# An expert layer on one core: all nodes at once in tiles of 256 rows, against two halves of the nodes in tiles of 128 rows

## The chip, the cores and the metric

The kernel runs on one core of one Trainium2 chip. The metric is the device time of one execution of the whole program, in microseconds (us). Three unprofiled runs of the kernel before took 3043.54, 3038.19 and 3040.16 us; their median, 3040.16, is the time before. The engines are named as in the profile: PE (TensorE matmul), PEld (TensorE weight load), DVE (VectorE), ACT (ScalarE), POOL (GpSimd) and SP (SyncE, which here only issues DMAs). A line number such as L1242 is a line of the kernel before, unless it is said to be of the changed kernel.

## What is computed

The input is a matrix x of 4096 nodes by 256 features and a 4096 x 4096 adjacency matrix. Layer 0 is a graph attention with 4 heads and a feed-forward part of 30 repeated steps; layer 1 is two graph attentions and then a mixture of experts. The change touches only this last part, and everything ahead of it stays as it was. Cut to that part, the reference is:

```python
n = layernorm(x)                                     # 4096 x 256
rh = relu(n @ router_w1 + router_b1)                 # 256 -> 128
p = softmax(rh @ router_w2 + router_b2)              # 128 -> 6 experts
top_w, top_i = top_k(p, 2)                           # two experts a node
w = softmax(top_w)
h1 = relu(n @ expert_w1[e] + expert_b1[e])           # each 256 x 256
h2 = relu(h1 @ expert_w2[e] + expert_b2[e])
y[e] = h2 @ expert_w3[e] + expert_b3[e]
x = x + w[0] * y[top_i[0]] + w[1] * y[top_i[1]]
```

The reference computes all six experts for every node; the kernel computes only the two that a node chose. All of it is in float32 except where the routing counts and compares small whole numbers.

## The kernel before, in words

P is 128, C is 256, KC is C/P = 2, E is 6 experts, G is 4. The 4096 nodes are 32 blocks of 128 (NT) or 8 groups of G x 128 = 512 nodes (NG, GR). The instructions are put in order on each engine by a scheduler that follows the order of the program's text as far as tiles and buffers allow; each engine then works through its own queue in order, and waits are semaphores. The expert stage (L938 to L1322) has three parts, one after the other.

**Routing.** The loop over groups (L971) is written as a pipeline. For a group it takes the rows of x (loaded by SP), finds mean and variance on DVE and the power -1/2 on POOL (`over_std`, L95 to L106), writes the normalised n on DVE (L992), stores n to the DRAM matrix nd through SP (L995), transposes n on PE into fT (L113, copied by ACT at L997), runs the router's two layers on PE (`ps_r` L981 with rh on ACT at L983, `ps_l` L1004), and adds the bias to the logits lg on DVE (L1007). ACT also keeps the group's rows in acc (L998), the sum that the outputs will be added to. After the eighth group SP issues the expert weights (18 transfers of 256 KB, L1016) and the last bias (L1017). Then some forty small DVE operations over all 32 blocks (L1054 to L1130) take the softmax, find the two best experts (`lmax`, `tot`, `top`, `hot`, `at`), count with matmuls by matrices of ones how many nodes each expert has ahead of a given one (`any` L1082, L1089 to L1092), find how many tiles each expert needs (`many` L1099), and give each of the 8192 pairs of node and choice a place in a list in which the pairs of one expert stand together and each expert begins at a new tile (`mine` L1121, then `pos`, `hi`, `lo`). The list is turned round by one-hot matrices: for four blocks of 16 x 128 pairs DVE writes `ohl` (L1137) and `ohh` (L1141, L1144), and PE multiplies them (L1147, 16 matmuls a block). From the product come `source`, the row of nd for each place (L1164), and `dest`, the row of yd (L1165). DVE then finds the expert of each tile (L1168 to L1176), the biases of its two hidden layers (`ohe`, `sel`, `bsel`, L1178 to L1188), and the two weights of each node (`ws`, L1191 to L1195).

**Tiles.** A tile is TR = 256 places of the list; T = 2 x 4096/256 + 5 = 37 tiles are enough for any choice of the nodes. For tile i:

- `gather`: POOL issues two indirect DMAs of 128 rows each from nd into gx (L1207; 4 buffers).
- `turn`: PE transposes gx into `pt` (L1219, 4 transposes), DVE copies it to xT (L1221).
- `fetch`: PE, DVE and ACT read the tile's expert number into a register (L1225); DVE copies that expert's first weight matrix and ACT the second to a fixed place (L1235).
- `hidden`, layers 0 and 1: PE multiplies (L1242, 4 matmuls of 256 columns a layer; the trace shows a float32 matmul as two records); relu with bias is on ACT for layer 0 (L1253) and on DVE for layer 1 (L1255).
- `result`: PE multiplies by the third matrix (`po`, L1263), DVE adds the bias (`ye`, L1271), and POOL issues two indirect DMAs that write the 256 rows to their places in the DRAM matrix yd (L1273).

The text interleaves two tiles, so that PE has another tile's work between two dependent steps:

```python
for i in range(T + 1):
    gather(i + 2)
    fetch(i + 1)
    hidden(i, 0, ...)      # PE, then ACT
    result(i - 1)          # PE, then DVE, then POOL
    turn(i + 1)            # PE, then DVE
    hidden(i, 1, ...)      # PE, then DVE
```

**Combine.** When all tiles are written, SP reads yd back in 16 transfers of 512 KB into y (L1308; 8 buffers), DVE adds each block of 128 rows, times its weight, to acc (L1319, 64 operations), and ACT issues the output of each group (L1322).

One row from outside the stage is spoken of too: L519 is the inner matmul of the attention (16-bit, 130 columns, a weight load for each), which is the last thing that runs ahead of this stage.

Of the kernel before, what the change touches and what calls it, by code (L numbers as in the profile page):

```python
# [11 lines left out]
F32 = mybir.dt.float32  # L12
# [11 lines left out]
P = 128  # L24
# [22 lines left out]
def gnn_ffn_kernel(ctx: ExitStack, tc: tile.TileContext, a: dict, out: bass.AP):  # L47
# [890 lines left out]
    with ExitStack() as scope:  # L938
        T = 2 * N // TR + E - 1
        T2 = 2 * T  # L940
# [4 lines left out]
        bsel = one.tile([P, T, 2 * KC], F32, name="bsel")  # L945
        expert = one.tile([P, T], I32, name="expert")
        dest = one.tile([P, T2], I32, name="dest")
        source = one.tile([P, T2], I32, name="source")
        ew = [one.tile([P, E, KC, C], F32, name=f"ew{i}") for i in range(3)]
        b3 = one.tile([P, E, C], F32, name="b3")  # L950
        nd = dram.tile([N, C], F32, name="nd")
        yd = dram.tile([2 * N + T * TR, C], F32, name="yd")

        with ExitStack() as rs:
            work = rs.enter_context(tc.tile_pool(name="r_work", bufs=2))
            rone = rs.enter_context(tc.tile_pool(name="r_one", bufs=1))
            psum = rs.enter_context(tc.tile_pool(name="r_ps", bufs=1, space=PSUM))
            ps_t = rs.enter_context(tc.tile_pool(name="r_pst", bufs=2, space=PSUM))

            def bank(name):  # L960
                return psum.tile([P, 512], F32, name=name)

            ps = bank("ps_s")
            nc.tensor.transpose(ps[:, :NB], br, ident[:NB, :NB])
            nc.vector.tensor_copy(bT, ps[:, :NB])

            lg = rone.tile([P, NT, E], F32, name="lg")
            rows, stds, fTs, rhs = {}, {}, {}, {}


            for g in range(NG + 2):  # L971
                if g + 2 < NG:
                    load_ahead(x3d, g + 2, runs_of)
                if g < NG:
                    rows[g] = ahead.pop(g)
                    stds[g] = over_std(work, rows[g])
                if 2 <= g:
                    ps = bank("ps_r")
                    fT = fTs.pop(g - 2)
                    for k in range(KC):  # L980
                        nc.tensor.matmul(ps[:RH], rw1[:, k, :], fT[:, k, :], start=(k == 0), stop=(k == KC - 1))  # L981
                    rh = rhs[g - 2] = work.tile([RH, GR], F32, name="rh")
                    nc.scalar.activation(rh, ps[:RH], AF.Relu, bias=bT[:RH, 0:1])  # L983
                if 1 <= g <= NG:
                    u = g - 1
                    t = rows.pop(u)
                    rstd, mv = stds.pop(u)
                    nmr = work.tile([P, G], F32, name="nmr")
                    nc.vector.scalar_tensor_tensor(nmr, mv[:, :, 0], -1.0, rstd, op0=OP.mult, op1=OP.mult)
                    n = work.tile([P, G, C], F32, name="n")  # L990
# [4 lines left out]
                    nc.sync.dma_start(runs_of(nd, u), n)  # L995
                    fT = fTs[u] = work.tile([P, KC, GR], F32, name="fT")
                    nc.scalar.copy(fT, transposed(ps_t, n))  # L997
                    nc.scalar.activation(acc[:, u * G : (u + 1) * G, :], t, AF.Identity, bias=mone)  # L998
# [14 lines left out]
            for i in range(3):  # L1013
                src = a[f"L1_ffn_expert_w{i + 1}"]
                for e in range(E):
                    nc.sync.dma_start(ew[i][:, e], src[e].rearrange("(k p) f -> p k f", p=P))  # L1016
            nc.sync.dma_start(b3, bcast_rows(a["L1_ffn_expert_b3"]))  # L1017

            def numbers(name, pattern, base, step, dtype=F32):
                shape = [P] + [n for _, n in pattern]  # L1020
                ti = rone.tile(shape, I32, name=f"{name}_i")
                nc.gpsimd.iota(ti, pattern=[list(x) for x in pattern], base=base, channel_multiplier=step)
                tf = rone.tile(shape, dtype, name=name)
                nc.gpsimd.tensor_copy(tf, ti)
                return tf

            HB = NT // 2
            along = numbers("along", [(1, max(T, N // TR))], 0, 0)
            along16 = numbers("along16", [(1, P), (0, HB)], 0, 0, F16)
            place = numbers("place", [(P, T2)], 2 * N + GR, 1)  # L1030


            code = rone.tile([P, 2, NT, 2], F16, name="code")
            nc.gpsimd.tensor_copy(code[:, :, :, 0], numbers("code0", [(0, 2 * NG), (1, G)], 0, G).rearrange(
                "p (i g) r -> p i (g r)", i=2))
            nc.gpsimd.tensor_copy(code[:, :, :, 1], numbers("code1", [(1, 2 * NG), (0, G)], 1, 0).rearrange(
                "p (i g) r -> p i (g r)", i=2))
            words = code.rearrange("p i t w -> p (i t w)").bitcast(F32).rearrange("p (i t) -> p i t", i=2)
            before = rone.tile([P, P], F32, name="before")
            nc.gpsimd.memset(before, 1.0)  # L1040
            nc.gpsimd.affine_select(
                before, before, pattern=[[1, P]], compare_op=OP.is_gt, fill=0.0, base=0, channel_multiplier=-1
            )
            before16 = rone.tile([P, P], BF16, name="before16")
# [242 lines left out]
        for i in range(T + 1):  # L1287
            if i + 2 < T:
                gather(i + 2)
# [63 lines left out]
```

## Time and profile before

| | |
|---|---|
| unprofiled runs | 3043.54, 3038.19, 3040.16 us; median 3040.16 |
| profiled execution, whole | 3026.16 us |
| its span, first to last instruction | 3024.4 us |
| mean granted clock of TensorE | 0.970 |
| busy PE, PEld | 2812.5 us (93%), 2549.3 us (84%) |
| busy DVE, ACT, POOL | 2709.9 us (90%), 2422.3 us (80%), 1167.0 us (39%) |
| expert stage in the trace | about 2690 to 3024.4 us |
| the list of rows to gather (`source`) complete | 2763.8 us |
| first gather; first hidden layer | 2764.80; 2772.2 us |
| first read of yd issued | about 2988.0 us |

The profile comes from one execution. Its times count from the first instruction; the whole is 1.8 us longer than the span. The busy shares are means over the whole program, most of which is the attention and the feed-forward part; the expert stage is its last tenth, so its limits have to be read from that stretch alone. The granted clock is the TensorE clock that the throttle gave, as a share of full speed. Matmuls are pipelined and the ends of the records are modelled, so the step from one record to the next is the length of a group of n records less the duration of one, divided by n - 1. A wait's releaser is inferred from semaphores, and where several semaphores are waited for, the one that came last by the profile is named.

### The profile page before, as it was taken

What the parts mean: (1) busy time and instruction counts of PE and PEld (TensorE: products, weight loads), DVE (VectorE), ACT (ScalarE), POOL (GpSimd) and SP (SyncE); (2) the same over time, 40 slices, a digit from 0 to 9 for tenths busy, and PEclk for the clock granted to TensorE, in tenths of its full rate; (3) what the DMA queues carried; (4) which work ended last, traced back from release to release, by engine and by line L of the source; (5) the groups of instructions that cost most, each with busy time, mean ns of one, the idle gap of its engine ahead of it and who ended that gap; (6) DMA issues with size and microseconds to landing.
All of it is one profiled execution on the core that took longest, in us unless ns stands there. A gap on an engine that the chain in (4) does not pass through costs nothing. (4 is left out here: it accounts for less than half of the span.)

```text
span 3024.4 us, 80903 instructions
## 1 busy us (share of the span) xinstructions
PE 2812.5 (93%) x33327; PEld 2549.3 (84%) x33327; DVE 2709.9 (90%) x5529; ACT 2422.3 (80%) x3011; POOL 1167.0 (39%) x1056
## 2 busy tenths in 40 slices
PE   6899999979999999999998999999799999985994
PEld 5899999958888888888877999999689999974883
DVE  8999999989999999999998899999689999985445
ACT  6799999788888888888867999999689999951220
POOL 2000000089999999999992000000200000022672
PEclk9999999989999999999999999999999999997997
DMA  9998884153333333333333022120302223142225
GB/s 291 273 247 242 231 247 114 33 134 68 68 68 69 67 67 70 68 67 69 69 100 109 29 93 85 41 89 16 106 27 86 71 92 93 30 137 76 95 93 200
DMA packets 482889, 319.96 MB, mean 106 GB/s; under 512 B 416573, under 2 KB 443354, under 8 KB 476378
## 3 DMA queue, kind: packets, MB, share of 16 engines
q1 hardware_dynamic: 467698, 287.13, 35.6%
q0 software_dynamic: 7680, 21.51, 2.2%
q10 hardware_dynamic: 7144, 6.16, 0.7%
q8 instruction: 263, 4.31, 0.6%
q14 instruction: 104, 0.85, 0.1%
HBM read 183.00 MB, written 52.04 MB: 78 GB/s over the span
## 5 line engine op out<-in xcount | busy, mean ns | idle before, releaser
L519 PE MATMUL acc<-vals,st 128*128 128x130 f16 x12288 | 1433.7, 219 | 35.7 <-DVE u L472 27.5
L519 PE MATMUL acc<-vals,below 128*128 128x130 f16 x12288 | 1433.3, 221 | 12.3 <-DVE below L573 11.7
L461 ACT ACTIVATE st<-f1b,nf 128x1024 int8<-128x1024 f32 x1265 | 1334.3, 1142 | 32.1 <-PE acc L519 22.7
L519 PEld LDWEIGHTS <-below 128*128 128x128 fp8e4 x12288 | 1177.1, 96 | 48.7 <-issue 44.1
L519 PEld LDWEIGHTS <-st 128*128 128x128 fp8e4 x12288 | 1208.8, 98 | 9.5 <-DVE st L567 7.5
L863 PE MATMUL po<-wT,zT 128*128 128x256 f32 x1920 | 576.0, 382 | 7.7 <-ACT zT L846 6.5
L866 PE MATMUL po<-w,zT 128*128 128x256 f16 x3840 | 577.7, 273 | 0.3 <-DMA zT<-z 0.3
L827 POOL TENSOR_TENSOR th<-th,y 128x1024 f32<-128x1024 f32 x240 | 567.6, 2365 | 26.8 <-ACT th L826 4.4
L866 PEld LDWEIGHTS <-zT 128*128 128x128 f16 x3840 | 376.3, 98 | 161.6 <-DMA zT<-z 1.3
L573 DVE TENSOR_TENSOR below<-m,st 128x1024 int32<-128x1024 int32 x384 | 469.9, 1224 | 32.7 <-DVE st L567 1.2
L567 DVE TENSOR_TENSOR st<-st,m 128x1024 int32<-128x1024 int32 x384 | 466.9, 1216 | 1.1 <-ACT st L461 0.9
L803 DVE SCALAR_TENSOR_TENSOR y<-po,z_rs,bias 128x256 f32<-128x256 f32 x928 | 384.4, 476 | 2.2 <-PE tp L796 0.7
L839 DVE BATCH_NORM_STATS2 z_st<-z 128x6 f32<-128x256 f32 x960 | 335.5, 411 | 0.0
L863 PEld LDWEIGHTS po<-wT,zT 128*128 128x128 f32 x1920 | 290.8, 192 | 17.7 <-ACT zT L846 9.3
L815 ACT ACTIVATE z<-th 128x1024 f32<-128x1024 f32 x240 | 251.0, 1046 | 8.6 <-POOL th L827 8.3
L826 ACT ACTIVATE th<-y 128x1024 f32<-128x1024 f32 x240 | 250.1, 1042 | 0.1
L105 POOL TENSOR_TENSOR ln_rstd<-ln_rstd,mhalf 128x4 f32<-128x4 f32 x24 | 32.0, 1334 | 562.0 <-ACT acc L998 491.8
L850 POOL TENSOR_TENSOR z_rs<-z_rs,mhalf 128x4 f32<-128x4 f32 x240 | 245.0, 1021 | 0.0
L846 ACT COPY zT<-tp 128x512 f32<-128x512 f32 x240 | 140.4, 585 | 110.3 <-PE tp L796 110.2
L459 DVE TENSOR_SCALAR st<-f1b,nf 128x1024 int8<-128x1024 f32 x271 | 200.9, 742 | 6.8 <-PE acc L519 6.8
L436 POOL MEMSET hs<- 128x4 f32 x3 | 0.3, 101 | 490.6 <-DVE u L489 490.6
L818 DVE SCALAR_TENSOR_TENSOR z<-z,scale,z 128x512 f16<-128x512 f32 x240 | 179.0, 746 | 4.9 <-ACT z L817 4.9
(237 smaller groups left out, 2815.4 us busy)
## 6 DMA issues: line engine op xcount, KB each, us to landing
adj<-in_adj_dram SPq DMA_DIRECT2D x64, 1024.0 KB
m<-edges SPq DMA_DIRECT2D x32, 1024.0 KB
f1b<-fd SPq DMA_DIRECT2D x48, 512.0 KB
edges<-m SPq DMA_DIRECT2D x16, 1024.0 KB
y<-yd SPq DMA_DIRECT2D x16, 512.0 KB
ew<-in_L_ffn_expert_w_dram SPq DMA_DIRECT2D x18, 256.0 KB
t<-in_x_dram SPq DMA_DIRECT2D x8, 512.0 KB
old<-in_x_dram SPq DMA_DIRECT2D x16, 256.0 KB
```

The source lines that it names most:

```text
L461: nc.scalar.activation(out, f1, AF.Sign, bias=f2, scale=-1.0)
L519: nc.tensor.matmul(acc[:, i, cols], masked[part][:, at_i // TR, s, rows], v[:, cols], start=(j == 0 and part == 0), stop=(j == NT - 1 and ...
L567: nc.vector.tensor_tensor(above, above, whole, OP.bitwise_and)
L573: nc.vector.tensor_tensor(below, whole, above, OP.bitwise_xor)
L803: nc.vector.scalar_tensor_tensor(y[:, g * G + r, :], po[:, r, :], rstd[:, r : r + 1], last if end else bias, op0=OP.mult, op1=OP.add,)
L815: nc.scalar.activation(z, th.pop(u), AF.Silu, scale=0.01)
L826: nc.scalar.activation(th[at], y[:, g * G : (g + 1) * G, :], AF.Tanh, scale=0.01)
L827: ins = nc.gpsimd.tensor_tensor(th[at], th[at], y[:, g * G : (g + 1) * G, :], OP.add)
L839: nc.vector.bn_stats(st[:, r, :], z[:, r, :])
L850: nc.gpsimd.tensor_tensor(rs[u], rs[u], mhalf, OP.pow)
L863: nc.tensor.matmul(po[:, r, :], src[:, r * P : (r + 1) * P], wT, start=True, stop=False)
L866: nc.tensor.matmul(po[:, r, :], src16[:, part * G + r, :], w16[:, other, :], start=False, stop=(part == 1 and other == 1),)
```

## The change

The nodes are cut into two halves of 2048 (NH), each of which has its own list, its own nd and yd, its own `source`, `dest`, `expert` and `bsel`. A tile becomes 128 places, so that a half has T = 2 x 2048/128 + 5 = 37 tiles, and both together 74. The stage's parts become:

- `route(h, ...)` is the routing of one half, written as a generator that stops at 20 places (`yield`). The half has 4 groups, 16 blocks, one-hot operations in two blocks instead of four, and about half as many elements in the small DVE operations. The constants that the routing needs are made once on POOL, ahead of it. The route of half 0 runs ahead of the tiles; after its first four steps SP issues the expert weights, so that they stand in SP's queue ahead of the stores of that half's last two groups.
- The route of half 1 takes one step after each tile of half 0 (`i < T - 2`); what is left of it is taken before the first gather of half 1.
- `combine(h)` is a generator too. That of half 0 takes one step after each tile from tile T + 5 on; what is left of it, and the combine of half 1, follow the tiles.
- In the tiles a gather, and a scatter, is one indirect DMA instead of two; `turn` has 2 transposes instead of 4, a layer of `hidden` has its 4 matmuls with 128 columns instead of 256, and `po` has 2 matmuls of 256 columns instead of 4. The w copies and the register reads stay as large as they were, so there are twice as many of them in all.
- Buffers: gx has 6 (of half the size) instead of 4, `ph` has 1 for each layer instead of 2, the second routing has a pool of one buffer for each of its two tiles in PSUM (`tp` and `ps`), and y has 4 instead of 8.

In the changed kernel's own queues, the gather of tile i + 8 stands next to the scatter of tile i on POOL; the four pow operations of the second routing stand between gathers 2 and 3, 3 and 4, 7 and 8, and after the first scatter. On DVE a tile is ye of tile i - 1, xT of i + 1, the register read and w copy of i + 2, then the two halves of h1 of i; the six one-hot operations of the second routing stand in one row ahead of a ye, and the first weighted sum of the first combine stands after xT of tile 40. ACT's four output issues of that combine stand after h0 of tiles 41, 43 and later ones.

The diff, cut to its core:

```diff
-        T = 2 * N // TR + E - 1
-        T2 = 2 * T
+        NH, NTH, NGH = N // 2, NT // 2, NG // 2
+        T = 2 * NH // P + E - 1
...
+        bsel = [one.tile([P, T, 2 * KC], F32, name=f"bsel{h}") for h in range(2)]
+        expert = [one.tile([P, T], I32, name=f"expert{h}") for h in range(2)]
+        dest = [one.tile([P, T], I32, name=f"dest{h}") for h in range(2)]
+        source = [one.tile([P, T], I32, name=f"source{h}") for h in range(2)]
...
+        nd = [dram.tile([NH, C], F32, name=f"nd{h}") for h in range(2)]
+        yd = [dram.tile([2 * NH + T * P, C], F32, name=f"yd{h}") for h in range(2)]
+        rwork = scope.enter_context(tc.tile_pool(name="r_work", bufs=2))
+        rone = scope.enter_context(tc.tile_pool(name="r_one", bufs=1))
...
+        def route(h, turned, bank):
+
+            lg = rone.tile([P, NTH, E], F32, name="lg")
...
+                    yield
+                if 1 <= g <= NGH:
...
+                    yield
...
+            for i in range(2):
+                ohh = rwork.tile([P, T, NTH], F32, name="ohh")
...
+                ohl = rwork.tile([P, P, NTH], F16, name="ohl")
...
+                        start=(i == 0 and t == 0),
+                        stop=(i == 1 and t == NTH - 1),
...
+            steps = route(0, turned, bank)
+            for _ in range(4):
+                next(steps)
+            for i in range(3):
+                src = a[f"L1_ffn_expert_w{i + 1}"]
+                for e in range(E):
+                    nc.sync.dma_start(ew[i][:, e], src[e].rearrange("(k p) f -> p k f", p=P))
+            nc.sync.dma_start(b3, bcast_rows(a["L1_ffn_expert_b3"]))
+            for _ in steps:
+                pass
...
-        ps_h = scope.enter_context(tc.tile_pool(name="m_psh", bufs=2, space=PSUM))
+        ps_h = scope.enter_context(tc.tile_pool(name="m_psh", bufs=1, space=PSUM))
         ps_o = scope.enter_context(tc.tile_pool(name="m_pso", bufs=2, space=PSUM))
+        ps_r = scope.enter_context(tc.tile_pool(name="m_psr", bufs=1, space=PSUM))
         rows, xT, hT, which, held = {}, {}, {}, {}, {}
-        scatters = []
+        scatters = [[], []]
...
         def gather(i):
-            rows[i] = work.tile([P, 2, C], F32, name="gx", bufs=4)
-            for r in range(2):
-                nc.gpsimd.indirect_dma_start(
-                    out=rows[i][:, r, :],
-                    out_offset=None,
-                    in_=nd[:, :],
-                    in_offset=bass.IndirectOffsetOnAxis(ap=source[:, 2 * i + r : 2 * i + r + 1], axis=0),
-                )
+            h, t = divmod(i, T)
+            rows[i] = work.tile([P, C], F32, name="gx", bufs=6)
+            nc.gpsimd.indirect_dma_start(
+                out=rows[i],
+                out_offset=None,
+                in_=nd[h][:, :],
+                in_offset=bass.IndirectOffsetOnAxis(ap=source[h][:, t : t + 1], axis=0),
+            )
...
+            for k in range(KC):
+                nc.tensor.matmul(po, src[:, k, :], w[:, 0, k, :], start=(k == 0), stop=(k == KC - 1))
...
+            y = work.tile([P, C], F32, name="ye")
+            nc.vector.tensor_tensor(y, po, b3[:, bass.DynSlice(which[i], 1)].rearrange("p o c -> p (o c)"), OP.add)
...
+        def combine(h):
+            ys = {}
+            for g in range(NGH + 2):
+                if g < NGH:
+                    ys[g] = []
+                    for i in range(2):
+                        ys[g].append(work.tile([P, G, C], F32, name="y", bufs=4))
+                        nc.sync.dma_start(ys[g][i], runs_of(yd[h], i * NGH + g))
+                    yield
+                if 2 <= g:
+                    at = (h * NGH + g - 2) * G
+                    for i, y in enumerate(ys.pop(g - 2)):
+                        for r in range(G):
+                            t = at + r
+                            nc.vector.scalar_tensor_tensor(
+                                acc[:, t, :], y[:, r, :], ws[:, i, t : t + 1], acc[:, t, :], op0=OP.mult, op1=OP.add
+                            )
+                        yield
+                    nc.scalar.dma_start(runs_of(out, h * NGH + g - 2), acc[:, at : at + G, :])
...
+        second = route(1, ps_r, lambda name: ps_r.tile([P, 512], F32, name="ps"))
         gather(0)
         gather(1)
-        for i in range(T + 1):
-            if i + 2 < T:
+        for i in range(2 * T + 1):
+            if i + 2 < 2 * T:
+                if i + 2 == T:
+                    for _ in second:
+                        pass
+                    second = combine(0)
                 gather(i + 2)
...
+            if i < T - 2 or i > T + 4:
+                next(second, None)
+        for _ in second:
+            pass
+        for _ in combine(1):
+            pass
```

## The prediction

> **What bounds the kernel now.** I read the page's slices first: only the last tenth of the span concerns this change, so I cut that tenth into stages with the table of busy time by stretch. Its columns are the stretch, its length, and busy time (instructions) of PE, PEld, DVE, ACT and POOL, then the granted clock, DMA share and GB/s.
>
> ```profile
> 2690.00:2729.00 39.00, 35.30 (x160) 21.91 (x160) 23.49 (x103) 18.17 (x21) 14.99 (x29) 0.88 0.82 283
> 2729.00:2744.50 15.50, 0.69 (x4) 0.27 (x4) 14.05 (x45) 0.59 (x2) 0.00 (x0) 0.53 0.07 27
> 2744.50:2764.80 20.30, 8.94 (x64) 8.31 (x64) 16.77 (x21) 0.77 (x2) 0.00 (x0) 0.58 0.00 0
> ...
> 2785.00:2983.00 198.00, 197.42 (x982) 173.40 (x980) 93.33 (x172) 49.52 (x103) 129.92 (x133) 1.00 0.28 89
> ...
> 2988.00:3024.40 36.40, 0.00 (x0) 0.00 (x0) 26.01 (x64) 0.00 (x0) 0.00 (x0) 0.50 0.88 346
> ```
>
> The reader is to see three serial stages: routing (to 2764.8), tiles (PE busy 197.4 of 198 us), and combine (DMA and DVE, no PE). Routing and combine leave PE nearly idle, but the tiles leave PE no room at all. The chain that ended last (start, length, what) gives the joints:
>
> ```profile
> 2727.64 1.07 PE ps_l L1004 x8
> ...
> 2744.54 1.30 DVE ohh L1141
> ...
> 2759.80 2.24 PE ps_r L1147 x16
> 2764.80 1.13 POOL gx L1207
> ...
> 2772.62 7.82 PE ph L1242 x24
> ...
> 2985.49 2.41 DMA yd<-ye,dest
> 2988.04 3.63 DMA y<-yd
> ...
> 3019.72 0.79 DVE acc L1319 x2
> ```
>
> In the tiles the chain runs over POOL's gathers and scatters, but each gather there waits for "PE pt"; the timeline of PE shows who leads. One tile of 256 rows:
>
> ```profile
> 2855.12 0.60 PE L1219 MATMUL pt<-ident,gx 128*128 128x128 f32 x4
> 2855.56 1.89 PE L1242 MATMUL ph<-h,w 128*128 128x256 f32 x8
> 2857.29 1.89 PE L1242 MATMUL ph<-xT,w 128*128 128x256 f32 x8
> 2859.02 1.89 PE L1263 MATMUL po<-ew,h 128*128 x8
> 2860.74 0.60 PE L1219 MATMUL pt<-ident,gx 128*128 128x128 f32 x4
> ```
>
> From pt to pt is 5.62 us, without a gap. One record's step is (group length − one duration)/(count − 1): (1.89 − 0.379)/7 = 0.216 for 256 columns, (0.60 − 0.273)/3 = 0.109 for a transpose of 128. DVE beside it:
>
> ```profile
> 2855.32 0.69 DVE L1271 TENSOR_TENSOR ye<-po,b 128x512 f32<-128x512 f32 x1 [1.16 <-DMA yd<-ye,dest]
> 2855.93 0.68 DVE L1221 COPY xT<-pt 128x512 f32<-128x512 f32 x1
> 2857.49 0.88 DVE L1255 TENSOR_SCALAR h<-ph,bsel 128x256 f32<-128x256 f32 x2 [0.88 <-PE ph L1242]
> 2859.22 0.56 DVE L1235 COPY w<-ew 128x512 f32 x1 [0.85 <-PE ph L1242]
> ```
>
> DVE works 2.8 of 5.62 us. ye starts 0.20 after po's last slot: with "DMA yd" named but PE just done, this wait is PE's.
>
> **The change, step by step** (on the profiled execution: span 3024.4, whole 3026.16 us).
>
> 1. Routing ahead of the tiles, now for half the nodes. The fourth group's lg stands at 2712.93, the eighth's at 2728.74: −15.8. Of the small DVE operations, some 16 of 192 elements (0.36) become 96 (0.26, as many L1099), and any and mine lose half of 1.0 and 0.87: −2.4; one w copy now stands among them, +0.6. The one-hot run, 2744.46 to 2759.74, was four blocks of 2 × 1.30 + 1.14; two blocks of 2 × 0.68 + 1.14 take 5.0: −10.3. Behind the one-hots the order by engine puts the second half's first statistics (4 × 0.35 + 3 × 0.1) between the list's last steps: +1.7. Sum **−26.2**. On SP, all 18 expert weight loads and the bias (5.5 MB) now precede two of the four nd stores. At 200 to 280 GB/s (the first stretch moved 283) they end near 2713, the stores a few us later, some 20 us before the first gather: nothing.
>
> 2. From the list to the first hidden layer: 8.4 us before (2763.8 to 2772.2). One gather less is needed for tile 0 (−1.4), but PE's queue has the transpose of tile 3 ahead of tile 0's second layer, and POOL now has a pow (1.05 + 0.30) between gathers 2 and 3. I take **0**, ends −2 and +4.
>
> 3. Tiles: 74 of 128 rows instead of 37 of 256, as many rows (9472), gathers (74) and scatters (74). Per tile PE has 16 hidden records of 128 columns, not in the trace as such. Below stands half of 0.216 = 0.108; above, each record's own weight load: L1004's, with 6 columns to stream, step (1.06 − 0.254)/7 = 0.115. I take 0.111: 1.78. po: 4 × 0.216 = 0.86; pt: 2 × 0.109 = 0.22. Sum 2.86, × 74 = 211.6 against 37 × 5.62 = 207.9: +3.7. The handovers do not halve. DVE after po's end: 0.20 to ye, 0.35 and 0.33 to get through ye and xT, some 0.2 for the register read (0.30 long) that the w copy needs, 0.49 for that copy, then h: first half ready at 1.92, and PE's weight load takes 0.18 more (first po: h at 2779.62, 0.48 long, po at 2780.28). PE's next po could start at 0.22 + 0.89 + 0.89 = 2.00. I charge 0.09 a tile: 2.95, +6.7. POOL needs 2 × (0.97 + 0.30) = 2.55 and stays under it. Sum **+10.4**; ends −1 (0.108, no wait) and +29 (3.20).
>
> 4. The second half's routing, placed among tiles 0 to 20. PE: per group 8 × 0.109 + 4 × 0.43 (L981) + 8 × 0.111 = 3.48, × 4 = 13.9; one-hots 32 × 0.14 = 4.5; counts 0.5. PE has no idle time there, so 18.9 is on the path: it is moved, not hidden. DVE: half of 23.5 + 14 + 16.8, with less saved on fixed costs, some 31 us. Idle DVE is about 1.0 a tile × 37 plus the time under PE's 18.9, so it fits by sum, but the queue is in order: the six one-hot operations (5.0) stand in a row ahead of a ye (+3), sel and bsel (0.99 each) ahead of h (+2), the counts wait for DVE (+1), small ones around xT (+3): +9. ACT's extra (four acc 1.15, eight fT 0.6, four rh 0.69) has room: it works under half of a tile. The four pow cost POOL 5.4 of its 14 idle us. Sum **+27.9**; ends +18.9 and +38.
>
> 5. The first half's combine, among tiles 39 to 47. 32 operations, 28 of which took 11.24 before: 0.40 each, 12.8 in 8 tiles, 1.6 a tile against 1.0 idle, partly ahead of h: +6. The first waits for its read: the last scatter (2.4 to land), then 3.6, while its place in DVE's queue is about two tiles after that po; what is queued behind it is h, and PE behind h: +3. SP has only later reads behind its wait; ACT's four output issues stand after h0 and before the next w copy. Sum **+9**; ends 0 and +15.
>
> 6. The end. The read back of one half: the first 8 of the 16 reads were used up by 3005.4 (the ninth group's wait ends at 3007.73), 17.4 after 2988.04, and then an output of 3.6 follows: 21.0 instead of 36.4, **−15.4**. Buffers fall from 8 to 4; with four in flight DVE (1.6 a read) still frees one before the next is due. Ends −18 and −11.
>
> Sum: −26.2 + 0 + 10.4 + 27.9 + 9 − 15.4 = **+5.7**: span 3030.1, whole 3031.9. The unprofiled runs had a median of 3040.16, 14.0 above the profiled one; I add the same difference: **3045.9**.
>
> Two rules of the Trainium skill speak against the change. In the L519 stream 479 records took 27.80 us, 0.058 each with a weight load for every 130 columns. "TensorE: Matmul & The Clock Gate", Back-to-back issue gap, gives 81 ns sustained at 128 columns against 56 isolated; by that surplus, 16 records × 25 ns would add an estimated 30 us to step 3. The row is this kernel's, so I leave it out. The w copy took 0.41 alone and 0.565 at the median among gathers, while those kept to 0.96 to 0.99: it is DVE that waits. "SBUF — State Buffer", the "DVE blocks DMA" trap, has it the other way: such a copy keeps GpSimd from writing descriptors; an estimated 0.43 on POOL's 2.55 would bound a tile at 2.98, 2 us more in all.
>
> **Rivals.** *Faster: the fillers fit.* DVE's 31 us and the combine go entirely into idle DVE time, and tiles run at 2.86. For it: idle time suffices by sum, and before, ye to h has 0.88 idle. Against it: the in-order blocks. −26.2 + 3.7 + 18.9 + 2 − 16 = −17.6: 3022.6. It decides if tiles 22 to 36 step at 2.9 or less and steps 4 and 5 lose under 5 us beyond PE's 18.9. *Slower: handovers bound the tile.* PE waits for h or xT in every tile because their latencies stay while the cover (0.89 instead of 1.73) halves; at 3.20 a tile step 3 grows by 18.5: +24, 3064. For it: my chain ends within 0.1 of PE's. It decides from about 3.05 on. *It doesn't do what it says:* the second list might end after tile 36 and hold gather 37. Its last steps are queued near tile 20, so 16 tiles (47 us) are spare; under 1 in 50, counted with slower.
>
> **How the numbers follow.** Chances: forecast 0.50, faster rival 0.28, slower rival 0.22. A measurement tells about 0.2%, 6.1 us, from no change. The forecast's own spread is ±8 around +5.7: of its 0.50, some 0.04 is faster, 0.23 within, 0.23 slower; its own range is 3038 to 3054. The faster rival gives 0.25 and 0.03, the slower 0.22. Faster 0.29, same 0.26, slower 0.45. The range takes in most of both rivals: 3024 to 3068.
>
> **What would show it.** Step 1: first gather near 2738. Step 3: pt to pt of 2.95 in tiles 50 to 70, hidden records at 0.111. Step 4: first to last po of the first half 28 us over 37 tiles' time, PE's gaps before h around the one-hots. Step 5: DVE idle before acc on "DMA y", stretched tiles 39 to 47. Step 6: 21 us from the last read's issue run to the end. I am wrong if hidden records step at 0.13 or more (weights not under the stream), or if PE falls to a lower granted clock between tiles, as it did after its idle time at 2764 (0.68 in that stretch).

## The result and the profile after

The changed kernel took 3031.83 us (median of 11 runs, 3027.09 to 3037.21) against 3040.16 (11 runs, one of which, 3312.09, stands far off): ratio 0.9972, 95% interval 0.9962 to 0.9982. It is faster by 8.3 us, where 5.7 slower was forecast; the time lies in the stated range, the sign is the other one. Its profiled execution has a span of 3033.0 and took 3034.78. So the two profiled executions stand the other way round than the medians: 3024.4 before, 3033.0 after. That contradiction is the first thing that had to be cleared up.

The table of busy time by stretch of the changed kernel; its columns are those of the prediction (stretch, length, busy time and instructions of PE, PEld, DVE, ACT, POOL, granted clock, DMA share, GB/s):

```profile
2713.00:2734.50 21.50, 3.08 (x36) 2.61 (x35) 19.59 (x72) 6.03 (x8) 0.00 (x0) 0.50 0.04 14
...
2741.60:2800.00 58.40, 58.23 (x392) 51.20 (x393) 35.49 (x118) 25.42 (x56) 31.53 (x32) 0.96 0.31 102
...
2919.00:2979.00 60.00, 55.63 (x394) 50.78 (x393) 31.63 (x90) 20.01 (x53) 35.34 (x36) 0.97 0.26 86
...
3010.00:3033.00 23.00, 0.00 (x0) 0.00 (x0) 13.11 (x32) 0.00 (x0) 0.00 (x0) 0.50 0.73 274
```

The reader is to see the same three kinds of stage, with the first and the last shortened (the list is ready at 2733.4, and only 32 sums follow the tiles), and a new thing in the third line: tiles with nothing placed among them, in which PE works 55.6 of 60 us. Before, that stretch had 197.4 of 198. The chain that ended last has the joints:

```profile
2734.55 1.13 POOL gx L1224
...
2883.87 3.84 DMA yd<-ye,dest
2887.73 3.28 DMA y<-yd
...
3007.53 2.41 DMA yd<-ye,dest
3010.88 6.20 DMA y<-yd
```

The first half's last scatter and first read now lie on the chain in the middle of the tiles (2883.87, 2887.73), the second half's at the end.

In PE's timeline, the starts of successive `po` are 2.87 apart where nothing disturbs a tile, but among tiles 50 to 65 the steps run 2.87, 2.97, 3.55, 3.5 and begin again; from tile 66 on, where no gather is left, every step but the last is 2.87. One of the long steps, PE (first fence), DVE (second) and ACT (third):

```profile
2966.15 1.03 PE L1281 MATMUL po<-ew,h 128*128 x4
2967.02 0.38 PE L1235 MATMUL pt<-ident,gx 128*128 128x128 f32 x2
2967.23 1.06 PE L1260 MATMUL ph<-h,w 128*128 128x128 f32 x8
2968.13 1.06 PE L1260 MATMUL ph<-xT,w 128*128 128x128 f32 x8
2969.70 1.13 PE L1281 MATMUL po<-ew,h 128*128 x4 [0.51 <-DVE h L1273]
```

```profile
2967.93 0.43 DVE L1252 COPY w<-ew 128x512 f32 x1
2969.29 0.61 DVE L1273 TENSOR_SCALAR h<-ph,bsel 128x128 f32<-128x128 f32 x2 [0.93 <-PE ph L1260]
```

```profile
2970.82 0.62 ACT L1271 ACTIVATE h<-ph,bsel 128x128 f32<-128x128 f32 x2 [3.28 <-PE po L1281]
```

PE's `ph<-h` ends by its records at 2968.29, and DVE, free since 2968.36, begins `h` at 2969.29. PE's `ph<-xT` ends at 2969.19, and ACT, idle for 3.28, begins at 2970.82, 1.6 later (in an undisturbed tile of the second run, after_again, it begins at 2953.06, 1.16 after the group's first record; here it is 2.7). PE's signals reach both of them late, and PE then waits 0.51 for what they hand back. As the ends of PE's records are modelled, the trace does not tell a late signal from a matmul that ended late; "late signals" below stands for either.

### The profile page after: what moved, and what is told of

Its sections match the earlier page's. It is cut to its first block, busy times and chain, and to the rows that moved or that the text cites. A ratio compares the mean times of both kernels' runs of the same rounds, so it can differ in the third digit from the quotient of the medians.

```text
span 3033.0 us, 82811 instructions
## 1 busy us (share of the span) xinstructions
PE 2824.9 (93%) x33923; PEld 2569.5 (85%) x33923; DVE 2739.1 (90%) x5766; ACT 2459.9 (81%) x3132; POOL 1167.7 (38%) x1056
## 5 line engine op out<-in xcount | busy, mean ns | idle before, releaser
L519 PE MATMUL acc<-vals,st 128*128 128x130 f16 x12288 | 1432.0, 218 | 36.1 <-DVE u L472 27.9
```

Source lines behind the costliest of these rows:

```text
L519: nc.tensor.matmul(acc[:, i, cols], masked[part][:, at_i // TR, s, rows], v[:, cols], start=(j == 0 and part == 0), stop=(j == NT - 1 and ...
```

## The experiments

The kernels of one batch ran on one chip, beside the kernel before. Times below are medians, with the ratio to the kernel before of that batch. Stage times are taken from the profiled executions: "ahead" is from the stage's first transpose to the first `pt`, "po to po" from the first `po` to the end of the last, "end" what follows.

### Batch 1: which profile was the odd one, and the change in parts (before: 3037.05)

**c_before**: no edit.

> The kernel before once more, unchanged. The two profiled executions say +8.6 (span 3024.4 to 3033.0), the medians say -8.3 (3040.16 to 3031.83). Theory A, the profiled execution of before was an unusual one ahead of the stage: here the expert stage (first transpose of its routing to the end) takes 334 +- 3 again, and the part ahead of it ends 12 to 15 us later than 2690.7. Theory B, it was unusual inside the stage: the part ahead ends at 2689 to 2692 and the stage takes 345 to 350, with the surplus in one of routing, tiles or combine. Theory C, neither: this profile has a span of 3023 to 3027 again while the median of the runs is near 3040; then the profiled execution and the other runs of this kernel differ always.

Measured: 3036.71, ratio 1.0 (0.9991 to 1.0009); span 3039.7. Theory B: the part ahead ends at 2692.4, the stage takes 347.3 instead of 333.7, and 10.9 of the surplus stand in po to po (213.9 instead of 202.9). The first step of `po` is 8.64 instead of 5.68, and from the fourth tile on, every second one is 6.0 to 6.2 long instead of 5.62, until the last gathers. PE and DVE in one of the latter:

```profile
2875.63 1.24 PE L1263 MATMUL po<-ew,h 128*128 x5
2876.71 0.60 PE L1219 MATMUL pt<-ident,gx 128*128 128x128 f32 x4
2877.14 1.89 PE L1242 MATMUL ph<-h,w 128*128 128x256 f32 x8
2879.32 1.99 PE L1242 MATMUL ph<-xT,w 128*128 128x256 f32 x8 [0.29 <-DVE xT L1221]
```

```profile
2877.98 0.69 DVE L1271 TENSOR_TENSOR ye<-po,b 128x512 f32<-128x512 f32 x1 [1.70 <-PE pt L1219]
2878.59 0.68 DVE L1221 COPY xT<-pt 128x512 f32<-128x512 f32 x1
```

`po` ends at 2876.87 and `ye` starts at 2877.98: 1.1 late, as in the changed kernel, and xT then comes too late for PE. In the profile of the prediction `ye` began 0.04 after the recorded end of `po` in all 37 tiles. So that profile came from an execution without the late signals, and the three runs shown beside it (3038 to 3044) were, by their times, of the kind that has them. The first tile of c_before is the worst, DVE and then PE:

```profile
2784.01 0.88 DVE L1255 TENSOR_SCALAR h<-ph,bsel 128x256 f32<-128x256 f32 x2 [5.86 <-remote]
```

```profile
2778.39 1.89 PE L1242 MATMUL ph<-h,w 128*128 128x256 f32 x8
2784.55 3.78 PE L1263 MATMUL po<-ew,h 128*128 x8 [3.41 <-DVE h L1255]
```

The `ph` that `h` reads ended at 2780.28, so `h` starts 3.7 late. PE then waits 3.41, and its records run at half speed for some 6 us (`po` 3.78 instead of 1.89): the granted clock was 0.50 there.

**tile128**: the kernel before with tiles of 128 rows, and nothing else.

```diff
+        TR = P
         T = 2 * N // TR + E - 1
-        T2 = 2 * T
+        T2 = T
...
-            rows[i] = work.tile([P, 2, C], F32, name="gx", bufs=4)
-            for r in range(2):
-                nc.gpsimd.indirect_dma_start(
+            rows[i] = work.tile([P, C], F32, name="gx", bufs=6)
+            nc.gpsimd.indirect_dma_start(
```

> The kernel before with tiles of 128 rows alone (69 tiles, no halves, nothing interleaved). In the changed kernel's trace an undisturbed tile took 2.87, but every fourth one lost about 1.5 while gathers ran. Theory A, the small tile itself brings that loss: 69 x 3.23 = 223 against 207.9, +15: about 3055. Theory B, the loss comes from what is placed among the tiles: 69 x 2.87 = 198, -10: about 3030.

Measured: 3034.64, ratio 0.9989 (0.9980 to 0.9998). Neither theory fits: the late signals are there (steps of 2.87 and 3.25 by turns, then 2.9, 3.5, 3.5, 2.87), po to po is 215.5, 3.1 a tile, and first `pt` to first `po` is 5.8 shorter than in c_before.

**halves_serial** and **combine_last**: the second routing, and the first combine, moved in the program's text.

```diff
 second = route(1, ps_r, ...)
+for _ in second:
+    pass
...
-            if i < T - 2 or i > T + 4:
+            if i < T - 2:
```

> The changed kernel with both routings ahead of the tiles and both combines behind them, 74 tiles of 128. Theory A, the interleaving pays: the second routing alone ahead costs about 36 instead of 28 in the tiles, and the first combine behind the tiles 13 instead of 9: +12 on the changed kernel, 3044. Rival: the fillers cost the tiles as much as they take alone: within 4 of the changed kernel, 3028 to 3036.

> The changed kernel with the first half's combine behind the tiles, the routing still among them. In its trace, tiles 37 to 51 took 13.5 more than 14 x 2.87, some 10 of it beyond the loss of every fourth tile. Theory A: 10 go, and 13 (32 weighted sums at 0.4, whose reads can run under the tiles) come back at the end: +3, 3035. Rival, the reads of the first half stand behind the last scatter on SP too, so that 17 come back: +7 or more, 3039.

Measured: 3036.73, ratio 0.9999 (0.9990 to 1.0008), and 3032.10, ratio 0.9979 (0.9970 to 0.9989). Neither kernel was what its edit says. The order of the instructions on DVE shows it: in combine_last (second edit alone) the sums of the first combine stand at tiles 38 to 46 as in the changed kernel, so this was a repeat of it; in halves_serial they still stand among the tiles (39 to 49), and of the second routing the matmuls stand ahead of the first `po` and the small operations and one-hots in a lump among the first six tiles. The scheduler, not the place in the text, decides. What halves_serial tells is that the lump costs 4.6 us against the drawn-out routing of combine_last: two steps of `po` there are 7.2 and 5.3, and from the first `pt` to the first `po` it takes 20.6 instead of 10.9.

### Batch 2: the changed kernel again, and plain transfers (before: 3025.58)

**after_again**: no edit.

> The changed kernel once more, unchanged, beside the kernel before on the same chip. By the stages of the second profile of before (routing to first gather 74.7, first to last po 213.9, end 41.3) and those of the changed kernel (45.9, 258.8, 26.2) the stage is 3.0 shorter, the medians say 8.3. Theory A, those 3.0 and 8.3 are the same number within the spread of single executions (10 us): a median 5 to 9 below before, and a profile whose po to po lies between 250 and 262. Rival: the profile of the changed kernel was a typical one and the medians' 8.3 is of other chips: 1 to 5 below before.

Measured: 3016.25, ratio 0.9967 (0.9955 to 0.9979), 9.3 below before; span 3017.4. Neither theory fits: this batch had no late signals at all, in before (3025.58, the time that belongs to the prediction's profile) as in the changed kernel, whose po to po is 239.0 instead of 258.8. Its tiles 50 to 65 take 0.3 more than 15 x 2.873. One of them, PE and then DVE:

```profile
2949.92 1.03 PE L1281 MATMUL po<-ew,h 128*128 x4
2950.79 0.38 PE L1235 MATMUL pt<-ident,gx 128*128 128x128 f32 x2
2951.01 1.06 PE L1260 MATMUL ph<-h,w 128*128 128x128 f32 x8
2951.90 1.06 PE L1260 MATMUL ph<-xT,w 128*128 128x128 f32 x8
2952.80 1.03 PE L1281 MATMUL po<-ew,h 128*128 x4
```

```profile
2950.99 0.42 DVE L1283 TENSOR_TENSOR ye<-po,b 128x256 f32<-128x256 f32 x1 [1.15 <-PE po L1281]
2951.33 0.42 DVE L1237 COPY xT<-pt 128x256 f32<-128x256 f32 x1
2951.94 0.43 DVE L1252 COPY w<-ew 128x512 f32 x1 [0.20 <-DVE xT L1237]
2952.28 0.60 DVE L1273 TENSOR_SCALAR h<-ph,bsel 128x128 f32<-128x128 f32 x2
```

PE steps 2.88 without a gap. On DVE, counted as in the prediction from the start of `pt` (2950.79, where `po`'s last slot ends), the first half of `h` is ready 1.83 later (2952.62, by a first half of 0.34). That is 0.18 before `po` starts (2952.80), which is when PE is through with the eight records of `ph<-xT` (2951.90 + 8 x 0.112).

**before_plain_gather, before_plain_scatter, after_plain_gather**: SP's plain transfers in place of POOL's indirect ones.

```diff
-                nc.gpsimd.indirect_dma_start(
-                    out=rows[i][:, r, :],
...
+                nc.sync.dma_start(rows[i][:, r, :], nd[at + r * P : at + (r + 1) * P, :])
...
-                ins = nc.gpsimd.indirect_dma_start(
-                    out=yd[:, :],
...
+                nc.sync.dma_start(yd[at : at + P, :], y[:, r, :])
```

> The kernel before with plain loads of 256 consecutive rows through SP in place of POOL's indirect gathers (so the tiles compute other rows than the list says; the list is made all the same). In the second profile of before every second tile takes 6.15 instead of 5.62, because a signal from PE to DVE, ACT or POOL comes about 1.1 late, and it stops with the last gathers. Theory A, the late signals come with the gathers: all tiles at 5.62, about 10 less than before, 3027. Rival, they come with the scatters or from PE itself: still 6.15, within 3 of before.

> The kernel before with plain stores through SP to consecutive rows in place of POOL's indirect scatters (so the rows of yd stand in the list's order and the sums take the wrong ones); the gathers stay. Theory A, the late signals come with the gathers: still there, though perhaps at other tiles; within 4 of before. Rival, they need the scatters: all tiles at 5.62, about 10 less, 3027.

> The changed kernel with plain loads of 128 consecutive rows through SP in place of the indirect gathers (other rows than the list says, the lists are made all the same). In its trace the tiles 57 to 65 took 3.24 on the mean against 2.87 after the last gather. Theory A, the loss comes with the gathers: 2.87 wherever nothing else is placed among the tiles, 74 x 0.3 = 15 to 22 less than the changed kernel, 3010 to 3017. Rival, the loss is of the handovers of a small tile or of the fillers: within 5 of the changed kernel.

Measured: 3020.75 (0.9982, 0.9973 to 0.9992), 2992.78 (0.9893, 0.9878 to 0.9909) and 3006.62 (0.9939, 0.9923 to 0.9954). As there were no late signals in this batch, nothing here tells where they come from. before_plain_scatter shows something else: with plain stores a read of yd waits only for its own rows, so the scheduler put all 64 sums among the tiles. The end shrinks from 41 to 4.1, and po to po grows only from 202.9 to 208.8.

### Batch 3: forced orders and loosened stalls (before: 3036.99, late signals)

**tile128_b**: as tile128.

> Tiles of 128 rows alone again (69 tiles, no halves, nothing interleaved), because its first profile was one with the late signals of PE that the second profile of the changed kernel (3017.4) does not have. Theory A, without them a small tile steps at 2.87 and no handover binds: 69 x 2.873 = 198 against 37 x 5.62 = 208, 8 to 11 below before. Rival, the small tile loses 0.3 in every session: 2 below before, as in its first run.

Measured: 3035.77, ratio 0.9993 (0.9984 to 1.0003); late signals again, po to po 215.7. It told nothing of a batch without them.

**route_ahead**: the second routing ahead of the first gather, this time by a dependence.

```diff
 second = route(1, ps_r, ...)
+for _ in second:
+    pass
+nc.vector.scalar_tensor_tensor(source[0], source[1], 0.0, source[0], op0=OP.mult, op1=OP.add)
```

> The changed kernel with the whole second routing ahead of the first gather, forced by a dependence (the first half's list gets zero times the second's added); halves_serial only asked for it in the text, and the order by engine shows that the second routing stayed among the first six tiles there and the combine among the second half's tiles. In the second profile of the changed kernel the second routing costs the tiles 20.0 (36 steps of po less 36 x 2.873). Theory A, ahead of the tiles it costs its chain: 15.8 for four groups, some 12 of small operations, 5 of one-hots, 2.5 of list, 36: 16 more than the changed kernel, some 7 above before. Rival, the two routings overlap one another there (one on PE, the other on DVE) and it costs no more than 24: within 4 of the changed kernel.

Measured: 3050.24, ratio 1.0047 (1.0032 to 1.0063), 13.3 above before. "Ahead" grows from 48.8 to 90.7, 41.8 for the second routing alone (36 were expected); po to po falls from 258.8 to 234.8. Theory A in kind, and its size was low: putting the routing among the tiles is worth some 22 us (13.3 above before against 8.3 below, of two batches).

**combine_end**: the first half's sums behind the last tile, by a dependence.

```diff
+                    nc.vector.scalar_tensor_tensor(
+                        held_back[g], y[:, : 2 * G].rearrange("p (i r) -> p i r", i=2), 0.0,
+                        ws[:, :, g * G : (g + 1) * G], op0=OP.mult, op1=OP.add,
+                    )
```

> The changed kernel with the first half's weighted sums behind the last tile, forced by a dependence (their weights get zero times the last tile's ye added); combine_last only asked for it in the text and its order by engine is that of the changed kernel, so that run was a repeat. In the second profile of the changed kernel this combine costs the tiles 8.3. Theory A: 8.3 go and 13 come back (32 sums at 0.40, their first four reads already in): 5 more than the changed kernel, 4 below before. Rival, the reads are what the end waits for: 17 more come back, so 9 more than the changed kernel, equal to before.

Measured: 3035.11, ratio 0.9995 (0.9986 to 1.0004). Against the profile after, which has late signals too, the end grows by 10.9 (37.1 instead of 26.2) and tiles 36 to 50 get back 7.9. By the medians it stands 6.4 above the changed kernel; theory A (5) and its rival (9) are not told apart by that.

**spread**: the one-hots a step each, the first combine's groups held back to tiles 41, 44, 47 and 50 in the same manner.

```diff
+                yield
                 nc.vector.tensor_tensor(ohh, ohh, words[:, i, None, :].to_broadcast([P, T, NTH]), OP.mult)
+                yield
...
+        LATE = [T + 4 + 3 * g for g in range(NGH)]
```

> The changed kernel with its two visible stalls loosened: the six one-hot operations of the second routing each with a step of its own (one to three a tile instead of six in a row; that row stretched a tile to 6.82), and the first combine's four groups held back by a dependence to the tiles 41, 44, 47 and 50, after their reads are in (the first sum's wait stretched a tile to 5.88). Theory A, the stalls are of the in-order queue of DVE: 3 of the 3.95 and 4 of the 8.3 go, 7 less than the changed kernel, some 16 below before (ratio 0.9945). Rival, the sums and one-hots take the same time from PE wherever they stand: within 2 of the changed kernel.

Measured: 3025.83, ratio 0.9956 (0.9942 to 0.9970). The long steps are gone, but not their time: the step of 6.83 became 3.14 and its neighbours grew, so that these five steps take 18.0 instead of 19.9. Tiles 36 to 50 take 4.9 more than undisturbed ones instead of 12.9; 2.6 of that difference stand at tiles 47 and 48, where the profile after has a late signal and no sum.

### Batch 4: the late signals (before: 3041.99, late signals)

> The kernel before with plain loads of consecutive rows through SP in place of the indirect gathers (other rows than the list says). Where the kernel before takes about 3037 beside it (late signals): Theory A, they come with the indirect gathers: all tiles at 5.62 and 10 to 16 below before; rival, they come from something else: tiles of 6.15 among those of 5.62, about 5 below before. Where before takes about 3025, there are none to remove: 4 to 6 below before, as in the first run.

> The changed kernel with plain loads in place of the indirect gathers (other rows than the lists say). Where before takes about 3037: Theory A, the late signals go with the gathers: steps of 2.87 in tiles 50 to 70 and 24 to 32 below before; rival, they stay: steps of 2.87 and 3.5 by turns and 14 to 18 below before. Where it takes about 3025: 19 below before, as in the first run.

> Tiles of 128 rows alone. Where before takes about 3037: 0 to 3 below before, as in its two runs. Where it takes about 3025: Theory A, no handover binds and a tile steps at 2.87, 8 to 11 below before; rival, the small tile still loses, 0 to 3 below.

> The changed kernel with the one-hots apart and the first combine held back to tiles 41 to 50. Where before takes about 3037: ratio 0.9956 again. Where it takes about 3025: Theory A, the loosened stalls are worth 7 beside the changed kernel's 9: 15 to 17 below before, 0.995; rival, the time is PE's in any place: 9 to 10 below, 0.9968.

The kernels are those of the earlier batches. Measured: **plain_gather_b** 3020.95, ratio 0.9934 (0.9917 to 0.9950), **after_plain_b** 3008.84, 0.9894 (0.9878 to 0.9911), **tile128_c** 3039.37, 0.9990 (0.9981 to 0.9999), **spread_b** 3030.21, 0.9964 (0.9951 to 0.9977). Without indirect gathers both kernels take the same time as in batch 2, to 0.2 and 2.2 us, while the kernel before went from 3025.58 to 3041.99. PE in a tile of plain_gather_b:

```profile
2878.95 0.60 PE L1215 MATMUL pt<-ident,gx 128*128 128x128 f32 x4
2879.39 1.89 PE L1238 MATMUL ph<-h,w 128*128 128x256 f32 x8
2881.12 1.89 PE L1238 MATMUL ph<-xT,w 128*128 128x256 f32 x8
2882.85 1.46 PE L1259 MATMUL po<-ew,h 128*128 x6
```

There is no gap, and all its tiles but the first and the last step at 5.62. In the changed kernel with plain loads (after_plain_b) tiles 50 to 65 step at 2.87, and it takes 33.2 less than before (24 to 32 forecast). That the batch had late signals is seen in the trace of tile128_c, whose steps are 2.87 and 3.3 by turns. Theory A holds: the late signals need the indirect gathers. Of the kernels that leave nothing out, spread is the fastest, but its two intervals overlap those of the changed kernel (0.9972, 0.9967): what it gains beyond it, 1 to 5 us by the ratios, is not settled.

## Why the prediction was wrong

Two pairs of profiled executions of the same kind can be set beside the sum: before's first profile with after_again (no late signals), and c_before with the profile after (late signals).

| step | forecast | without late signals | with |
|---|---|---|---|
| 1. routing ahead, to the first gather | -26.2 | -28.2 | -28.9 |
| 2. to the first hidden layer | 0 | -0.6 | -0.6 |
| 3. tiles of 128 rows | +10.4 | +5.9 | |
| 4. second routing in the tiles | +27.9 | +19.9 | |
| 5. first combine in the tiles | +9 | +8.8 | |
| 3 to 5 together | +47.3 | +34.6 | +41.5 |
| 6. the end | -15.4 | -14.5 | -15.0 |
| sum | +5.7 | -8.7 | -3.0 |

(Step 4 is the first 36 steps of `po` less 36 x 2.873, step 5 the same for the rest without the last, shorter step, step 3 what remains of the way from the first hidden layer to the last `po`. With late signals the three can't be parted.) The cuts at both ends were priced within 2.7. The error is in the tiles: of 14.4, 4.5 in step 3, 8.0 in step 4.

**Step 3, the charge of 0.09 a tile for handovers, failed.** The PE part was right: hidden records step at 0.112 (0.111 taken), and 16 x 0.112 + 4 x 0.216 + 2 x 0.109 is the 2.87 that was measured. The charge was the chain on DVE, 1.92, and 0.18 for PE's weight load, less the 2.00 at which PE could start. Both terms were too long. In tiles 46 to 69 of after_again the first half of `h` is ready at 1.66 to 1.86 (one tile excepted: 57, at 2.14, whose step is 3.05), since the w copy passes on after 0.34 to 0.39 and not 0.49. The 0.49 came from copies of 0.565, the median of that one profile; in c_before and in the changed kernel the median is 0.43. The 0.18 was a misreading. It was taken at the first `po` of before, but PE was not waiting there:

```profile
2779.42 1.03 PE L1242 MATMUL ph<-xT,w 128*128 128x256 f32 x4
2780.28 1.96 PE L1263 MATMUL po<-ew,h 128*128 x8
```

The four records of `ph<-xT` fill PE until 2779.42 + 4 x 0.216 = 2780.28. Where a `po` does wait for `h`, as at 2886.70 below, it starts 0.05 to 0.06 after the first half is done. So the handover is over at about 1.9, ahead of 2.00, and PE sets the tile. The charge was 6.7 in all; 2.873 is 0.013 over the 2.86 of PE's records, 1.0 in all. (The other 1.2 of step 3 lie outside these steps, at the first and the last tile.)

**Step 4, both terms were too large.** PE's own share was taken as 18.9; counted in after_again between the first half's first and last `po` it is 15.7 (`ps` of L1010 in the changed kernel 6.9, router logits 3.25, transposes 3.1, one-hots 2.3 at 0.073 a record instead of 0.14, counts 0.1), since a group's transposes come before the first `po` and the one-hots of 74 columns were charged as those of 148. The stalls were taken as 9, the remainder is 4.2: 2.3 of it are idle time of PE in tiles 13 to 18, around the one-hots, the rest are records that step a little slower. DVE and then PE in after_again:

```profile
2813.55 0.77 DVE L1130 TENSOR_TENSOR ohh<-along,hi 128x592 f32<-128x592 f16 x1
2814.24 1.22 DVE L1135 TENSOR_TENSOR ohl<-along,lo 128x2048 f16<-128x2048 f16 x1
2815.37 0.77 DVE L1133 TENSOR_TENSOR ohh<-ohh,code 128x592 f32<-128x592 f32 x1
2816.06 0.77 DVE L1130 TENSOR_TENSOR ohh<-along,hi 128x592 f32<-128x592 f16 x1
2816.74 1.22 DVE L1135 TENSOR_TENSOR ohl<-along,lo 128x2048 f16<-128x2048 f16 x1
2817.88 0.77 DVE L1133 TENSOR_TENSOR ohh<-ohh,code 128x592 f32<-128x592 f32 x1
2818.57 0.42 DVE L1283 TENSOR_TENSOR ye<-po,b 128x256 f32<-128x256 f32 x1
```

```profile
2816.20 1.25 PE L1140 MATMUL ps<-ohh,ohl 128*128 128x74 f16 x16
2818.70 1.26 PE L1140 MATMUL ps<-ohh,ohl 128*128 128x74 f16 x16 [1.25 <-DVE ohh L1133]
```

The row of six and the place ahead of `ye` are as forecast. But while DVE is busy for 5.0, PE does half of the one-hot matmuls, transposes and hidden layers of the next tile, and idles for 1.25, not 3. The price of 3 left PE 2.0 of other work under a block of 5.0; it had 3.75.

**Step 5 was right in sum, in part by luck.** In after_again DVE waits for the first read and PE behind it; DVE, then PE, then the stretch that follows:

```profile
2885.78 0.48 DVE L1310 SCALAR_TENSOR_TENSOR acc<-y,ws,acc 128x256 f32<-128x256 f32 x1 [3.15 <-DMA y<-yd]
2886.30 0.61 DVE L1273 TENSOR_SCALAR h<-ph,bsel 128x128 f32<-128x128 f32 x2
```

```profile
2886.70 1.93 PE L1281 MATMUL po<-ew,h 128*128 x4 [2.85 <-DVE h L1273]
2888.85 1.75 PE L1260 MATMUL ph<-h,w 128*128 128x128 f32 x8
```

```profile
2887.00:2890.00 3.00, 3.00 (x12) 2.52 (x12) 2.93 (x8) 0.00 (x0) 0.67 (x1) 0.50 0.98 385
```

The step of `po` there is 5.88, 3.0 too long (3 forecast). The next step is 4.63, 1.8 too long, though PE has no idle time in it: after the wait the granted clock was 0.50, and `po` took 1.93 instead of 1.03, `ph<-h` 1.75 instead of 1.06. The prediction named a lower clock between tiles as a sign that it was wrong, but had no term for it. The steps at the other sums, tiles 40 to 45, are 3.7 too long where 6 were forecast, and tiles 57 and 58 add 0.3. So the sums were priced too high, and the slow clock made up for most of it. Steps 1, 2 and 6 were right; step 1 gained 2 more than forecast.

**The basis.** The prediction added 14.0 to both kernels for the gap between before's profile and its median. The gap was real, and c_before, another execution of the same kernel, shows where such a gap lies: 12.9 us between the first hidden layer and the last `po` (223.7 instead of 210.8), 4.9 of them up to the second `po` (the 3.7 of the late `h` and the slow records after it), the other 8.0 in the tiles of 6.0 to 6.2. The prediction left the gap unexplained and took it for the same in both kernels. By the medians of the batches that was near the truth: late signals go with 11.4 to 16.4 before (3036.99 to 3041.99 against 3025.58) and 15.6 after (3031.83 against 3016.25). By one execution each it is 12.9 before and 19.8 after (265.2 instead of 245.4), so that the two profiles with late signals give -3.0 where the runs give -8.3. The basis did not turn the sign of the sum, but two profiles of different kinds, before without and after with late signals, gave the +8.6 of the first comparison.

**The rivals.** The faster one (-17.6) had the tiles right, which step at 2.87, and the result (-8.3, later -9.3) lies nearer to it than to the forecast; but its other condition (steps 4 and 5 lose under 5 us beyond PE's 18.9) was not met: they lost 9.8, and the combine kept its 8.8. The slower one, handovers at 3.20, did not occur without late signals, and with them the step of 3.2 came from elsewhere: the tiles of the kernel before lengthen as well, and both are cured by plain gathers. The chances leant to the slower side because three uncertain terms (0.09 a tile, 9 of stalls, the one-hot price) all erred to the same side.

**The two rules of the Trainium skill.** By "TensorE: Matmul & The Clock Gate", Back-to-back issue gap, an estimated 30 us were to come on top at 128 columns; the records step 0.112, about half of the 0.216 of 256 columns, so no run here shows it. For the trap "DVE blocks DMA" of "SBUF — State Buffer" an estimate of 2 us was given, for the w copies; beside these no run here shows such a hold: POOL's gathers and scatters have a median of 0.98 in the profile after and 0.99 before. Beside the row of one-hots one may be seen. POOL in after_again:

```profile
2813.40 0.98 POOL L1224 DMA_INDIRECT gx<-nd,source  x1 [0.31 <-PE ph L1260]
2816.28 3.21 POOL L1224 DMA_INDIRECT gx<-nd,source  x1 [1.90 <-PE pt L1235]
```

The second gather takes 3.21 and begins while DVE is in that row; the profile after has the same gather at 3.22. What it cost the tiles was not measured.

## What to carry to other kernels

Work moved under a busy engine costs that engine's own share in full (15.7 here) and the wait of an in-order queue only so far as the other engine's queue is empty meanwhile: price a block on DVE by what PE has queued behind it, not by its length. A wait that leaves PE idle for 2 us or more can cost more than its length, by the clock that follows it (1.8 after 2.85 here). Before a profiled execution is taken as the base of a sum, explain the gap to the median of the runs: 14 us of 3040 were larger than the whole effect, and they lay in the very stage that was changed. A move in a program's text that a scheduler orders is not an experiment until the order on the engine shows it; a dependence (zero times the value to wait for) makes it one.

## What the runs showed of the hardware

Beside indirect gathers of POOL, PE's signals to DVE, ACT and POOL came late in some batches, mostly by 0.9 to 1.6 us, in single places by 2.7 (after, the `h` at 2926.34) and 3.7 (c_before, 2784.01); once in two tiles of 256 rows, once in two or four of 128, and not at all in another batch of the same kernels. They ended with the last gather, and plain loads of the same size through SP removed them. By the medians of the batches, which ran on several chips, they go with 11.4 to 16.4 us in the kernel before and 15.6 in the changed one. What delays them, why some batches have none (the record names chip 0 for batch 1, with them, and for batch 2, without), and whether the scatters would do the same are not settled: the plain scatters ran only where there were no late signals.

Among the tiles, six waits of PE of 1.96 to 3.41 us (one in c_before, two in after, one each in after_again, after_plain_gather and after_plain_b) all brought a granted clock of 0.50, for 3.5 to 7 us; of the shorter ones, 1.2 to 1.9 us, some did (combine_last, 1.86) and some did not (after, 1.92). A float32 weight load of 128 x 128 for every 128 columns stayed hidden under the stream (0.112 a record).
